# Layer 0's projections in float32r halves, five buffers of exponentials, and the FFN's halves made in the attention's last quads

## The chip, the core and the metric

The kernel runs on one core of one Trainium2 chip. The metric is the device time of one execution in microseconds (us). Five engines work side by side and wait for each other by semaphores: TensorE (PE, matmuls and transposes, with its weight loads as PEld), VectorE (DVE), ScalarE (ACT), GpSimd (POOL), and SyncE (SP), which here only issues DMAs.

## The reference: what is computed

Two transformer layers over x with B = 8 sequences of S = 512 rows and D = 256 columns, 16 heads of 16:

```python
x = x + _L0_attn_ref(_layernorm(x), gamma, beta, w_qkv)      # causal attention
x = x + _L0_ffn_ref(_layernorm(x), w_gate, w_up, w_down)     # gated FFN, 704 wide, fp4-quantized
x = x + _L1_attn_ref(_layernorm(x), Wq, bq, Wk, bk, Wv, bv, Wo, bo)  # causal, window of 64
x = x + _L1_ffn_ref(_layernorm(x), w_gate, w_up, w_down)     # gated FFN, 768 wide, integer weights
```

In layer 0's attention, `xn = (x - mu) * rsqrt(var + eps) * gamma + beta` and `qkv = xn @ w_qkv.T`; then the softmax of causal scores, and the weighted sum of v. In layer 0's FFN inputs, weights and hidden rows are each quantized to fp4 by blocks of 16 with the block's largest value as scale. A small change of q, k or the FFN's input can tip a quantized value, so the kernel keeps nearly full fp32 precision.

## The kernel before

x stays in SBUF for the whole kernel as eight tiles X[b] of 128 x 4 x 256. The work falls into an opening (0 to 38 us in the profiled execution), layer 0's attention (38 to 500), layer 0's FFN (to 797), layer 1's attention (to 1100) and layer 1's FFN.

**Attention.** `attention()` (line 360) gives an `opening` and a `body`. A batch is two units m (eight heads each), a unit two quads g of four heads: 32 quads. The loop of line 775 goes over the quads i, with r = i % 4 the quad of the batch. A quad of layer 0 has six positions p. At each, in this order, the loop emits one tile of the scores of quad i + 2 (`scores`: matmuls of lines 501 and 506 into a PSUM pair s, DVE's maximum in line 517), one tile of the transposed scores of quad i (`Outputs.causal`: matmuls of line 609 into a PSUM pair t, ACT's exponential in line 620 into a buffer "ex", POOL's causal selection in line 128), and what `at(p, ...)` has put beside it:

- the sums of ex with the values, line 674: key blocks 2 and 3 of the quad before at p1 = 1, key blocks 0 and 1 of this quad at f3 = 5; ACT's copy oT (695), the transposes pot (702), and x's update (1003, 1005);
- per batch, at r = 0 the values v (`values`) and the statistics of batch c + 2, at r = 1 its normalization y (168), at r = 2 its transposition (`turned`, `spin0`, `transposed`: PE 185, ACT 196 with gamma and beta as scale and bias into yT), at odd r the projections q and k of a later unit (`load_q`, `load_k` through `pieces`), and their ways through HBM (`stores`, `land`);
- the rows of maxima (567, 577, 578).

`step()` gives a turn to a filler in 3 of 10 calls: `before_ffn` quantizes layer 0's FFN weights (220 to 282), transposes them (884, 901), prepares the FFN's input of batch 0, and as its last steps splits gate weights, up weights and that input into halves (967 to 970). What is left of it runs after the loop.

PE's matmuls and transposes of the attention are pinned: their order is that in which the code emits them. The other engines' orders come from a scheduler that puts instructions by estimated times; pools with a number of buffers decide when a tile may be written again. All ex tiles of layer 0 share NX = 6 buffers, a quad has six of them. psum1 tiles share two buffers of one PSUM bank, psum2 tiles three pairs.

**Projections.** `project` (297) is two fp32 matmuls (one for each 128 rows of the contraction); each runs as two passes of 128 columns of weights in the profile, so q and k take four passes of 512 columns for a unit, v four of 256 for each 128 rows. Layer 1, from its second batch, uses the halves: a number is split in a float32r high part and a float32r rest, and `PAIRS` multiplies high x high, high x low and low x high, one pass each.

**Units' tiles.** `units_tiles` (349) makes a unit's q and k tiles and copies rows of constants (`own`) into k (353) on DVE; it is called twice in the opening and once in each `body`.

**Layer 0's FFN** begins with `wd_halves` (1204 to 1211): ACT copies the high half of the down weights (128 x 1536), POOL subtracts (line 1209). It then goes over 32 tiles of 128 rows; `prepare(1)` makes the input of batch 1 (`normed`: statistics, then ACT's fy in line 168).

Of the kernel before, what the change touches and what calls it, by code (L numbers as in the profile page):

```python
# [19 lines left out]
P = 128  # L20
# [7 lines left out]
NX = 6  # L28
# [18 lines left out]
def tile_two_layers(  # L47
# [51 lines left out]
    qkv_raw = wp.tile([P, NE, 3 * D], F32, tag="raw", name="qkv_raw")  # L99
    w3 = w_qkv_t.rearrange("(c p) f -> p c f", p=P)  # L100
    for i in range(3):
        nc.scalar.dma_start(qkv_raw[:, :, i * D : (i + 1) * D], w3[:, :, i * D : (i + 1) * D])
# [74 lines left out]
    def transposed(dst, src, tag, cs=range(NE), cols=None, pinned=False):  # L177
# [4 lines left out]
        for c in cs:  # L182
# [7 lines left out]
            if low is not None:  # L190
                nc.scalar.copy(dst[:, c, :], pt)
                nc.vector.tensor_tensor(low[:, c, :], pt, dst[:, c, :].bitcast(F32), ALU.subtract)
            elif cols is None:
                evacuate(dst[:, c, :], pt)
            else:
                nc.scalar.activation(
                    dst[:, c, :], pt, AF.Identity, bias=cols[1][:, c : c + 1],
                    scale=cols[0][:, c : c + 1],
                )

    def quantize(pool, dst, src, rows, nb, tag, exact):
# [29 lines left out]
        else:  # L231
# [15 lines left out]
            q8, pr = tmp("q8", BF16), tmp("pr")  # L247
# [49 lines left out]
    def project(dst, lhs, rhs):  # L297
# [3 lines left out]
        for l, r in pairs:  # L301
            for e in range(NE):
# [46 lines left out]
    def units_tiles(pool, n, what):  # L349
# [3 lines left out]
        nc.vector.tensor_copy(  # L353
# [4 lines left out]
    QK = [units_tiles(qk, n, "both") for n in range(2)]  # L358

    def attention(home, banded, stats, norm, spin, wq_s, wk_s, wv_s, qcol, kcol, bv_bc, post, filler):  # L360
# [11 lines left out]
        def halved(i, b, w):  # L372

            return [x[:, i] for x in FINE["qkv"]] if banded and b else [w]
# [26 lines left out]
        def pieces(b, m, w, col, name):  # L401
# [3 lines left out]
            project(pp, [x[:, :, m * P : (m + 1) * P] for x in ws], xT[b])  # L405
# [63 lines left out]
        def turned(b, c):  # L469
            if c == 0:  # L470
                fine = banded and b
# [4 lines left out]
                if fine:  # L476
# [267 lines left out]
        def body():  # L744

            q, k = units_tiles(home[0], 2, int(banded))
# [27 lines left out]
            ending = filler(home[0]) if banded else None  # L774
            for i in range(len(quads) + (2 if banded else 1)):
# [49 lines left out]
                if cur and not banded:  # L825
                    at(f3, lambda: cur.sums((0, 1)))
# [6 lines left out]
                for p in range(max(len(ts), nT if last or done else 0)):  # L833
# [10 lines left out]
                    if banded and i > 4 * B - 6:  # L844
# [4 lines left out]
            for _ in ending or ():  # L849
                pass  # L850
# [99 lines left out]
    def before_ffn(pool):  # L950
# [7 lines left out]
        pool.release()  # L958
        high = HALVES["pool"] = tc.alloc_tile_pool(name="halves", bufs=1, side="right")
        for t, nm, homes in (  # L960
            (wg1, "wg", (high, high)), (wu1, "wu", (high, high)), (YT[0], "y", (wp, wp)),
        ):
# [506 lines left out]
```

## Time and profile before

| | us |
|---|---|
| runs: median (lowest to highest) | 1281.98 (1281.46 to 1284.03) |
| profiled execution, whole | 1288.33 |
| its span | 1286.5 |
| layer 0's attention, 38 to 500: PE busy | 403.2 of 462 |
| the same: DVE, ACT, POOL busy | 376.3, 274.4, 239.7 |
| mean granted clock of PE | 0.954 of full speed |

A line of the timeline reads: start, duration of the group, engine, line of the code, operation, result <- operands, tile sizes and type, how many in a row, and in brackets how long the engine stood idle before it and what ended that. A "wait" line names the engine, what it was about to do, and the work whose end released it. Matmuls overlap, so that the time of a block of passes is best read from the start of its first to the start of PE's next work.

### The profile page before, as it was taken

What the parts mean: (1) busy time and instruction counts of PE and PEld (TensorE: products, weight loads), DVE (VectorE), ACT (ScalarE), POOL (GpSimd) and SP (SyncE); (2) the same over time, 40 slices, a digit from 0 to 9 for tenths busy, and PEclk for the clock granted to TensorE, in tenths of its full rate; (3) what the DMA queues carried; (4) which work ended last, traced back from release to release, by engine and by line L of the source; (5) the groups of instructions that cost most, each with busy time, mean ns of one, the idle gap of its engine ahead of it and who ended that gap; (6) DMA issues with size and microseconds to landing.
All of it is one profiled execution on the core that took longest, in us unless ns stands there. A gap on an engine that the chain in (4) does not pass through costs nothing. (4 is left out here: it accounts for less than half of the span.)

```text
span 1286.5 us, 27214 instructions
## 1 busy us (share of the span) xinstructions
PE 1100.3 (86%) x10910; PEld 819.8 (64%) x10910; DVE 943.5 (73%) x1603; ACT 659.7 (51%) x1008; POOL 698.8 (54%) x821
## 2 busy tenths in 40 slices
PE   4778989788998888788888887788998898889998
PEld 2444444444554445787888777567777776668887
DVE  4699896698788885789799857677776686545553
ACT  3255656465674676444444333455555554455553
POOL 5165564465445566655555533576766675534443
PEclk9899999898998999899999988899999998999999
DMA  8644334443453311000000025476675676000001
GB/s 229 140 96 87 86 74 86 79 94 67 91 116 74 81 18 50 1 1 1 1 1 1 1 72 105 100 165 155 144 149 125 141 164 163 2 1 33 33 26 43
DMA packets 51634, 99.53 MB, mean 77 GB/s; under 512 B 6702, under 2 KB 43568, under 8 KB 44848
## 3 DMA queue, kind: packets, MB, share of 16 engines
q1 hardware_dynamic: 50624, 96.96, 33.9%
q8 instruction: 88, 1.44, 0.5%
q10 hardware_dynamic: 816, 0.79, 0.2%
q14 instruction: 42, 0.34, 0.1%
q0 software_dynamic: 64, 0.00, 0.0%
HBM read 61.02 MB, written 29.36 MB: 70 GB/s over the span
## 5 line engine op out<-in xcount | busy, mean ns | idle before, releaser
L128 POOL TENSOR_SCALAR_AFFINE_SELECT ex<-ex 64x512 f32<-64x512 f32 (+2 forms) x448 | 268.9, 603 | 226.1 <-ACT ex L620 131.3
L620 ACT ACTIVATE ex<-t 128x1024 f32<-128x1024 f32 (+1 forms) x192 | 167.9, 882 | 125.3 <-PE t L609 114.1
L517 DVE TENSOR_REDUCE mx<-s 128x2 f32<-128x1024 f32 (+2 forms) x192 | 196.7, 1036 | 41.1 <-PE s L506 40.3
L1319 POOL TENSOR_TENSOR hT<-gh,hT 128x512 fp32r<-128x512 f32 x48 | 61.6, 1290 | 89.6 <-ACT hT L1318 66.1
L655 ACT ACTIVATE ex<-t 128x1024 f32<-128x1024 f32 x64 | 65.5, 1023 | 86.6 <-PE t L647 81.9
L501 PE MATMUL s<-kk_both,qq_both 96*128 96x512 bf16 (+3 forms) x352 | 84.6, 323 | 20.8 <-DVE mx L517 10.9
L506 PE MATMUL s<-cmask,minus_b 128*128 128x128 bf16 (+2 forms) x352 | 90.4, 257 | 0.0
L540 DVE TENSOR_REDUCE mx<-s 128x8 f32<-128x1024 f32 x64 | 77.6, 1215 | 15.3 <-PE s L535 15.2
L282 POOL TENSOR_TENSOR h<-h,sc_h 128x704 f32<-128x704 f32 x32 | 45.1, 1410 | 79.4 <-DVE h L281 73.6
L674 PE MATMUL po<-ex,vp 128*32 128x512 f32 (+3 forms) x1024 | 83.4, 442 | 1.3 <-DVE kr L418 1.3
L609 PE MATMUL t<-qq_both,kk_both 108*128 108x512 bf16 (+3 forms) x352 | 70.9, 306 | 9.1 <-ACT ex L620 4.7
L1386 DVE SCALAR_TENSOR_TENSOR gh<-ggu,gsl 128x512 f32<-128x512 f32 x48 | 33.2, 691 | 57.1 <-ACT gsl L1384 56.6
L1260 PE MATMUL pd<-wd_high,hT 128*128 128x256 f32 x384 | 61.7, 299 | 11.6 <-DVE hT L1251 7.0
L277 ACT ACTIVATE mg_h<-h 128x704 bf16<-128x704 f32 x32 | 25.2, 788 | 82.7 <-POOL h L229 82.7
L1227 PE MATMUL gu<-wg_wgh,fyT 128*128 128x352 f32 x224 | 65.3, 333 | 2.4 <-DVE h L1234 2.4
L501 PEld LDWEIGHTS <-qq_both 96*128 96x128 bf16 x352 | 33.0, 103 | 51.6 <-issue 38.0
L229 POOL TENSOR_TENSOR h<-h,rc_h 128x704 f32<-128x704 f32 x32 | 46.4, 1449 | 34.1 <-DVE rc_h L228 18.8
L1260 PEld LDWEIGHTS pd<-wd_high,hT 128*128 128x128 f32 x384 | 53.7, 200 | 16.4 <-DVE hT L1251 10.7
L1227 PE MATMUL gu<-wu_wuh,fyT 128*128 128x352 f32 x224 | 62.7, 322 | 0.0
L1375 PE MATMUL ggu<-yT,wg_r 128*128 128x512 f32 x192 | 57.6, 412 | 2.1 <-DVE yT L1319 1.1
L279 DVE SCALAR_TENSOR_TENSOR h<-mg_h,h 128x704 f32<-128x704 bf16 x32 | 40.6, 1269 | 22.4 <-ACT mg_h L277 22.4
L674 PEld LDWEIGHTS po<-ex,vp 128*32 128x32 f32 x1024 | 27.1, 109 | 43.9 <-issue 29.8
(335 smaller groups left out, 3167.9 us busy)
## 6 DMA issues: line engine op xcount, KB each, us to landing
q_hbm<-qp SPq DMA_DIRECT2D x90, 128.0 KB
k_hbm<-kp SPq DMA_DIRECT2D x90, 128.0 KB
qq_both<-q_hbm SPq DMA_DIRECT2D x44, 256.0 KB
kk_both<-k_hbm SPq DMA_DIRECT2D x22, 384.0 KB
qq_both<-q_hbm SPq DMA_DIRECT2D x44, 128.0 KB
kk_both<-k_hbm SPq DMA_DIRECT2D x22, 256.0 KB
qq<-q_hbm SPq DMA_DIRECT2D x20, 256.0 KB
vq<-vp SPq DMA_DIRECT2D x8, 512.0 KB
```

Of the source, the lines that this page charges most:

```text
L128: nc.gpsimd.affine_select(out=t, in_=t, compare_op=ALU.is_ge, fill=0.0, base=base, pattern=[[0, n] for n in shape[1:-1]] + [[sign, shape[- ...
L501: pin(nc.tensor.matmul(bank[:, a * w : (a + 1) * w], lhsT=q[:KF, hs[j], t * P : w], rhs=k[:KF, hs[j], :w], start=(a == 0), stop=False, ski ...
L506: pin(nc.tensor.matmul(bank.rearrange("p (i k) -> p i k", k=w)[:, :, t * P :], lhsT=minus_b, rhs=cmask[:, : len(part), :], start=False, st ...
L517: nc.vector.tensor_reduce(dst, src, AX.X, ALU.max)
L540: nc.vector.tensor_reduce(mx[:, t2 : t2 + 2, :], sc.rearrange("p t (j k) -> p t j k", k=P), AX.X, ALU.max)
L609: pin(nc.tensor.matmul(bank[:, a * w : (a + 1) * w], lhsT=k[: KF + 12, self.hs[j], t * P : (t + 1) * P], rhs=q[: KF + 12, self.hs[j], t * ...
L620: nc.scalar.activation(ex[:, :banks, :used], sc[:, :banks, :used], AF.Exp, scale=QSCALE)
L655: nc.scalar.activation(ex, sc, AF.Exp, scale=QSCALE)
L674: pin(nc.tensor.matmul(self.o[HP * j : HP * (j + 1), t * P :], lhsT=vp[:, t, 4 * c + j, :], rhs=self.ex[t, j], start=(t == 0), stop=(t == ...
L1227: nc.tensor.matmul(gu[:, i, :352], lhsT=YT[b][l][:, e, t * P : (t + 1) * P], rhs=w[r][:, e, f], start=(n == 0), stop=(n == 3 * NE - 1),)
L1260: nc.tensor.matmul(pd[:, :D], lhsT=hT[l][:, k, :], rhs=wd_halves[r][:, k, :], start=(l == r == k == 0), stop=(l == 1 and k == NH - 1),)
L1319: engine.tensor_tensor(lo, src, hi.bitcast(F32), ALU.subtract)
```

## The change

Names and sizes in the diff: KF = 96 rows of a unit's tiles, "raw" a place of the weights' pool that held `qkv_raw`.

- The qkv weights come into three ex buffers and are split into float32r halves in the opening (ACT copies, DVE subtracts). `transposed` writes the scaled and shifted block to a full tile, copies its high half (ACT) and subtracts (POOL; for batch 0 DVE). The projections of layer 0 then take three pairs, with q's and k's low half of the input last (`last`; in layer 1 too).
- NX goes from 6 to 5, and the quantizer's q8 shares the buffer of mg.
- The sums of key blocks 0 and 1 go from position f3 = 5 to f2 = 4.
- The constants' rows are copied by ACT in the opening and by POOL in `body`, in both layers.
- The FFN's halves become a generator `ffn_halves` of their own. It is stepped at positions 2 and 5 of the quads from i = 27, and its first step runs the filler to its end. It makes the down weights' low half too, in three pieces.

```diff
-NX = 6
+NX = 5
...
-    qkv_raw = wp.tile([P, NE, 3 * D], F32, tag="raw", name="qkv_raw")
-    w3 = w_qkv_t.rearrange("(c p) f -> p c f", p=P)
-    for i in range(3):
-        nc.scalar.dma_start(qkv_raw[:, :, i * D : (i + 1) * D], w3[:, :, i * D : (i + 1) * D])
...
-            if low is not None:
+            if low is not None and cols is not None:
+                full = cols[2]()
+                nc.scalar.activation(
+                    full, pt, AF.Identity, bias=cols[1][:, c : c + 1], scale=cols[0][:, c : c + 1]
+                )
+                nc.scalar.copy(dst[:, c, :], full)
+                cols[3].tensor_tensor(low[:, c, :], full, dst[:, c, :].bitcast(F32), ALU.subtract)
+            elif low is not None:
...
-            q8, pr = tmp("q8", BF16), tmp("pr")
+            q8, pr = tmp("mg", BF16), tmp("pr")
...
-    def project(dst, lhs, rhs):
+    def project(dst, lhs, rhs, last=False):
...
         for l, r in pairs:
+            if last:
+                l, r = r, l
...
-    def units_tiles(pool, n, what):
+    def units_tiles(pool, n, what, copy=nc.vector.tensor_copy):
...
-        nc.vector.tensor_copy(
+        copy(
             k[KF:].bitcast(F32), own[KF:].unsqueeze(2).to_broadcast([32, 8, S // 2])
         )
...
-    QK = [units_tiles(qk, n, "both") for n in range(2)]
+    QK = [units_tiles(qk, n, "both", nc.scalar.copy) for n in range(2)]
...
-            project(pp, [x[:, :, m * P : (m + 1) * P] for x in ws], xT[b])
+            project(pp, [x[:, :, m * P : (m + 1) * P] for x in ws], xT[b], True)
...
-                fine = banded and b
+                fine = not banded or b
...
-                if fine:
+                if not banded:
+                    xT[b].append(home[0].tile([P, NE, S], F32R, tag="yT0", name=f"yTl_{b}", bufs=1))
+                elif b:
                     xT[b].append(FINE["x"])
...
-            q, k = units_tiles(home[0], 2, int(banded))
+            q, k = units_tiles(home[0], 2, int(banded), nc.gpsimd.tensor_copy)
...
-            ending = filler(home[0]) if banded else None
+            ending = last_weights(home[0])
...
-                    at(f3, lambda: cur.sums((0, 1)))
+                    at(f2, lambda: cur.sums((0, 1)))
...
-                    if banded and i > 4 * B - 6:
+                    if i > 4 * B - 6 and (banded or p % 3 == 2):
                         next(ending, None)
...
+        qkv = [
+            wp.tile([P, 3, NE, D], F32R, tag=f"raw{n}", name=f"qkv_{n}") for n in ("", "l")
+        ]
+        for i in range(3):
+            full = ap.tile([P, 2, 512], F32, tag="ex", name=f"qkv_{i}", bufs=NX)[:, :, :D]
+            nc.scalar.dma_start(
+                full, w_qkv_t[:, i * D : (i + 1) * D].rearrange("(c p) f -> p c f", p=P)
+            )
+            QKV.append([wqkv[:, i] for wqkv in qkv])
+            halved.append((QKV[i], full))
+
+        def split_weights(i):
+            (high, low), full = halved[i]
+            nc.scalar.copy(high, full)
+            nc.vector.tensor_tensor(low, full, high.bitcast(F32), ALU.subtract)
...
         def spin0(b, c, dst):
-            transposed(dst, Y[b], f"a{b}", [c], (gcol, bcol), True)
+            if b == 0:
+
+                for i in range(3) if c == NE - 1 else ():
+                    split_weights(i)
+
+            def full():
+                return ap.tile([P, S], F32, tag="rem", name=f"yf_{b}_{c}")
+
+            engine = nc.gpsimd if b else nc.vector
+            transposed(dst, Y[b], f"a{b}", [c], (gcol, bcol, full, engine), True)
+
+        def ffn_halves(pool):
+
+
+            for _ in fill:
+                pass
+            wqp.release()
+            high = HALVES["pool"] = tc.alloc_tile_pool(name="halves", bufs=1, side="right")
+            for t, nm, homes in (
+                (wg1, "wg", ((high, "wgh"), (high, "wgl"))),
+                (wu1, "wu", ((high, "wuh"), (wp, "rawl"))),
+                (YT[0], "y", ((wp, "wg1"), (wp, "wu1"))),
+            ):
+                hi, lo = HALVES[nm] = [
+                    h.tile(list(t.shape), F32R, tag=tag, name=f"{nm}_{tag}") for h, tag in homes
+                ]
+                for e in range(NE):
+                    nc.scalar.copy(hi[:, e], t[:, e])
+                    nc.gpsimd.tensor_tensor(lo[:, e], t[:, e], hi[:, e].bitcast(F32), ALU.subtract)
+                    yield
+            YT[0] = HALVES["y"]
+            low = HALVES["wd"] = wp.tile([P, NH, D], F32R, tag="raw", name="wd_low")
+            for k in range(0, NH, 2):
+                hi = pool.tile([P, 4, D], F32R, tag="y", name=f"wd_high_{k}", bufs=1)[:, :2]
+                nc.scalar.copy(hi, wd1[:, k : k + 2])
+                nc.gpsimd.tensor_tensor(
+                    low[:, k : k + 2], wd1[:, k : k + 2], hi.bitcast(F32), ALU.subtract
+                )
+                yield
...
         wd_halves = [
-            wp.tile([P, NH, D], F32R, tag="raw", name="wd_high"),
-            fp.tile([P, NH, D], F32R, tag="wdl", name="wd_low", bufs=1),
+            fp.tile([P, NH, D], F32R, tag="wdh", name="wd_high", bufs=1), HALVES["wd"]
         ]
         nc.scalar.copy(wd_halves[0], wd1)
-        nc.gpsimd.tensor_tensor(
-            wd_halves[1], wd1, wd_halves[0].bitcast(F32), ALU.subtract
-        )
```

## The prediction

> **What bounds the kernel now.** I read the page's busy shares and slices first, then the stages' windows, PE's waits, and last the rows of the projections.
>
> ```profile
> PE 1100.3 (86%) x10910; PEld 819.8 (64%) x10910; DVE 943.5 (73%) x1603; ACT 659.7 (51%) x1008; POOL 698.8 (54%) x821
> PE   4778989788998888788888887788998898889998
> DVE  4699896698788885789799857677776686545553
> ```
>
> PE is the busiest engine, but few slices of layer 0's attention (slices 2 to 15, 32 us each) are full, and DVE comes close behind. The windows say it for the stage from 38 to 500 us (columns: time, then busy us of PE, its weight loads, DVE, ACT, POOL):
>
> ```profile
> 38.00:500.00 462.00, 403.23 (x2994) 220.14 (x2994) 376.34 (x631) 274.35 (x384) 239.68 (x322) 0.94 0.38 80
> ```
>
> PE works 403.2 of 462 us (87%). So PE work that goes is mostly time saved, and the 59 us in which PE stands still are the second thing the change can move. What ends them (us in total, times, longest):
>
> ```profile
> PE s L501 <- DVE mx L517: 17.2, 17, 3.3
> PE t L609 <- DVE mx L517: 9.8, 16, 1.8
> PE t L609 <- ACT ex L620: 9.7, 9, 3.6
> PE pot L702 <- ACT oT L695: 8.6, 6, 4.0
> ```
>
> DVE's maximum reduces free the score buffers too late (27 us), and ACT's exponentials and copies come late (18 us). That is a chain through three engines with PE's order written by hand; no wait is on a load of the weights.
>
> **Part 1: the projections, six passes of halves for four of fp32.** The old passes in layer 0, and the new kind as layer 1 already has it:
>
> ```profile
> 263.60 1.88 PE L303 MATMUL pk<-yT,qkv_raw 128*128 128x512 f32 x4
> 265.32 0.39 PE L501 MATMUL s<-kk_both,qq_both 96*128 96x128 bf16 x4
> ...
> 898.01 0.74 PE L303 MATMUL pq<-yT,qkv_wg 128*128 128x512 f32 x2
> 898.59 0.63 PE L303 MATMUL pq<-room,qkv_wg 128*128 128x512 f32 x2
> 899.05 0.62 PE L303 MATMUL pq<-yT,qkv_wu 128*128 128x512 f32 x2
> 899.54 0.66 PE L702 MATMUL pot<-ident,oT 128*128 128x128 f32 x4
> ```
>
> From the first pass to the next work of PE: 265.32 - 263.60 = 1.72 us before, 899.54 - 898.01 = 1.53 us in halves. Over all blocks of the trace the medians are 1.72 against 1.53 (q), 1.72 against 1.59 (k), 1.73 for eight passes against 1.53 for twelve (v). A batch has two of each: 2 x (0.19 + 0.13 + 0.20) = 1.04 us; seven batches lie in the loop: 7.3 us of PE. Bounds: the passes of one block in layer 1 follow each other in 0.235 us (512 columns) and 0.119 us (256), so six blocks without any start-up loss would gain 6 x 0.31 = 1.8 us a batch, 12.8 us. On the other side, a weight load of these lines lasts 0.188 us; if loads set the pace, twelve take 2.26 us against 1.73, which is +0.53 for each v block, and with q and k still gaining 0.64 a batch the part would cost 7 x 0.42 = 2.9 us. I take the measured blocks, 7.3, since it is the same shape on the same engine. Not all of it comes through: where DVE or ACT is the late one, a shorter block only makes the wait longer. The share of PE's busy time, 0.87, is the upper end; with 27 of 59 idle us ended by DVE I take 0.75: **-5.5**.
>
> A rule speaks against this part. The Trainium skill, "Perfetto Trace Analysis", section "Identifying the Most-Contended Engine", would have TensorE judged by the busy share of its weight loads and not of its matmuls; the change raises layer 0's from 32 to 48 loads a batch, and by 0.188 us each that is 3 us a batch, about 21 us slower. The rows of layer 1 disagree: twelve loads and passes went through in 1.53 us, so the loads overlap.
>
> **Part 2: the price of the halves of yT.** Before, one ACT pass (L196, 0.77 us) moved a transposed block out of PSUM; after, the pass writes a full copy, ACT copies its high half (a 128x512 copy is 0.58 to 0.63) and POOL subtracts (128x512 in f32, 1.16 to 1.27; in batch 0 DVE, 0.68). Per batch ACT +1.2, POOL +2.5 us; ACT is busy 59% and POOL 52% of the stage, so most of it lies beside PE. What doesn't:
> - The wait. PE's order has pq pinned soon after the transposes. In batch 2 the transposes end at 97.13, ACT's pass at 98.17, pq starts at 99.81: 1.64 us of room. The added copy, subtract and hops need 0.6 + 1.25 + 0.2 = 2.05; but x-low comes last, four passes or 1 us after pq's start. So it fits when POOL is free (room 2.6), and when POOL is in a select (0.41 to 0.70) or a product of the quantizer (1.92 at 256.07) it is late. Behind the waiting pass stand all the scores and tiles of PE. Ends: 0, and 2.5 us a batch; I take 0.3, by the selects: 6 x 0.3 = **+1.8**. At the loop's start (50 to 54 us) pq follows the transposes at once (51.82, with yT ending at 52.49), nothing covers the chain: 2.05 less what the passes hide: **+1.8** (0 to 4).
> - ACT's 1.2 us delays exponentials; with 18 us of PE's waits ended by ACT in 274 busy us, 7 x 1.2 more cost 8.4 x 18/274 = 0.6, twice that at the worst: **+1.0**.
>
> **Part 3: opening (0 to 38 us).** DVE's copies of own rows, one of them from 8.13 to 9.79, go to ACT and POOL. DVE's statistics then end earlier, and y, which starts at 14.62 after an ACT that stood still 9.77 us, at some 12.8. Against it: the extra ACT passes (+1.2) and three splits of weights beside it. Six passes save again. The first scores at 38.51 wait for k's way through HBM, which keeps its length. **-1.0** (-2 to +1).
>
> **Part 4: five buffers, sums one position earlier.** The first half of a quad's sums (16 passes) needs four exponentials, and it then stands before the sixth tile, which takes the buffer that it frees: no new wait by count. Their 1.7 us of passes now stand ahead of the sixth tile, where PE waited 0.4 to 1.2 us in about ten quads, 6 us in all, and no longer ahead of the next quad's scores. I take half: **-3** (-4 to +2, if the fourth exponential is late and the sixth tile with it).
>
> **Part 5: the FFN's halves.** The same six copies (ACT) and subtracts (POOL) move from after the loop's last steps into the last five quads; the down weights' low half, one POOL subtract of 3.51 us at 501.93 beside which a DVE instruction stretched to 2.16 us, becomes three pieces of 0.6 (ACT) and 1.2 (POOL) in the loop. What is freed at FFN0's start is 1.4 to 1.8 us of DVE; but the ACT copy of the high half (1.48 us) now stands right ahead of the normalization of batch 1 on ACT: **-0.3** (-1.8 to +1.5).
>
> **Part 6: layer 1's start (797 to 805 us).**
>
> ```profile
> 797.97 2.51 DVE L353 COPY kk<-own 32x2048 f32<-32x2048 f32 x1
> ...
> 804.71 1.22 PE L303 MATMUL pq<-yT,qkv_wg 128*128 128x512 f32 x2 [3.68 <-DVE room L192]
> ```
>
> The copy stands on DVE ahead of the reduces, the rows of maxima and the low half of x (room), for which PE waits 3.68 us. It goes to POOL (2.5 us earlier), and x-low is read two passes later (0.5). What comes next is ACT's high half, so not all: **-3** (-3.7 to 0).
>
> **Part 7: the order.** The scheduler moves the quantizer's steps. In the changed order one quad (batch 4, third quad) has between two of DVE's reduces some 8.4 us of other work, with batch 6's statistics, two waits for POOL and the transposes behind y; before has such a place at 293 to 305, where 13 us held 8.64 us of PE. After such gaps PE also runs slower: from 238 to 262, with PE idle 3.34 and 3.97 us, the granted clock was 0.81. The old jams stay or go by accident: **+1.5** (-3 to +6).
>
> **Sum:** -5.5 + 1.8 + 1.8 + 1.0 - 1.0 - 3 - 0.3 - 3 + 1.5 = -6.7 us. The profiled execution took 1288.3 us (span 1286.5), so 1281.6 there. It is 6.35 us above the median of the runs (1281.98), which makes **1275.3**.
>
> **Rivals.**
> 1. No change: the stage is set by the DVE chain (81% busy, 27 us of PE's waits), so PE's savings only lengthen waits: part 1 gives 0, and the sum is -1.2: 1281. For it: every slice's DVE digit of 6 to 9; against it: PE is busy 87% and has the fewest idle us.
> 2. Much faster: passes at their spacing (12.8 x 0.87 = 11.1), all of part 4 (-4), no order cost, yT's wait covered except at the start: -11.1 + 1.8 + 1.0 - 1 - 4 - 0.3 - 3 = -16.6: 1265.
> 3. Slower: yT's low half on POOL is the new wait of every batch. It queues behind two selects or a product (1.2 to 1.9 us) and PE stands behind the pinned pass. At 2.5 us a batch it is 15 in place of 1.8: -6.7 + 13.2 = +6.5: 1288. It decides from 0.3 + 6.7/6 = 1.4 us a batch. For it: DVE and POOL both wait for each other around y (mr_a took 1.89 us beside a POOL product at 256.13); against it: room of 2.6 us.
>
> **How the numbers follow.** Forecast (1271 to 1279) 0.42, rival 2 and beyond 0.18, rival 1 0.16, rival 3 0.24. Runs of this kernel tell 0.2% (2.6 us) from no change. The forecast and rival 2 are faster (0.60); rival 1 mostly the same (0.14 of 0.16), the rest with rival 3 slower (0.26). The range leaves out the far halves of both ends: 1263 to 1289.
>
> **What would show it.** Right: blocks of six in layer 0 at 1.5 to 1.6 us; the loop 5 to 10 us shorter between 38 and its end; PE's waits for the sixth tile gone; no PE wait for room at layer 1's start above 1.2 us. Wrong: a PE wait "pq or pk for POOL yTl" that sums over 8 us, an 8 us hole in batch 4, blocks of 2 us, or waits for the maxima that grow by what part 1 saved.

## The result, and the profile after

The changed kernel takes 1287.1 us (median of 12 runs, 1283.6 to 1295.2), the kernel before 1282.2 (12 runs, 1275.6 to 1284.0): a ratio of 1.0046, 95% interval 1.0028 to 1.0064. It is 3.6 to 8.2 us slower where I forecast 6.7 us faster. The busy times of the changed kernel:

```profile
PE 1095.3 (85%) x11038; PEld 829.4 (65%) x11038; DVE 940.8 (73%) x1604; ACT 677.2 (53%) x1032; POOL 723.4 (56%) x839
```

PE has 5 us less to do, ACT and POOL 18 and 25 us more. In the window of layer 0's attention it shows most clearly:

```profile
38.00:500.00 462.00, 396.50 (x3076) 225.51 (x3076) 376.34 (x631) 282.63 (x399) 265.78 (x338) 0.93 0.39 81
```

PE was busy 403.2 us there and is now 396.5; DVE is as busy as it was. A part of these 6.7 us is only the window, in which all now comes later. Between the same instructions (first exponential of the first and of the last quad, 56.55 to 491.71 us before and 61.16 to 494.31 now) PE was busy 379.5 us and is now 374.6: 4.9 less, in a time that is 2.0 us shorter. PE's waits, 40 to 495 us (the 9.8 us for k belong to the opening; before, this wait of 8.5 us ended ahead of 40):

```profile
PE s L504 <- DVE mx L520: 18.9, 17, 4.0
PE t L612 <- DVE mx L520: 10.4, 10, 3.7
PE s L504 <- DMA kk_both<-k_hbm: 9.8, 1, 9.8
PE pt_a L181 <- ACT y L164: 8.9, 1, 8.9
PE t L612 <- ACT ex L623: 7.3, 16, 1.8
...
PE pq L304 <- ACT yT L191: 2.0, 5, 1.4
PE pq L304 <- POOL yTl L192: 1.7, 6, 0.4
```

Whole spans mislead here: both profiled executions of the kernel before took 1288 us, 6 over its median, with 294 and 295 us in layer 1's attention, where the others took 286 to 291 (less and more, below: 296 and 298). So I cut each trace at the same instructions. The table gives us from the span's start to the first exponential of layer 0, on to the first exponential of the 32nd quad ("loop"), to the FFN's first gate, through the FFN's gates, to layer 1's first exponential, through its exponentials, and to the end. The last columns are the medians of the runs and the ratio to the kernel before on the same chip.

```
kernel         first  loop   to FFN  FFN    to L1  L1 att.  rest    median   ratio (95%)
before          56.5  435.2   13.6  274.1   33.9   293.6   179.5    1282.2
before_again    56.6  434.8   13.6  274.1   33.9   294.9   178.5
after           61.2  433.2   16.2  272.8   31.4   289.3   179.9    1287.1   1.0046 (1.0028-1.0064)
after_again     61.2  434.5   16.2  272.8   31.4   289.9   179.5
stats_early     60.3  435.8   16.2  271.9   28.8   287.6   179.5    1284.3   1.0010 (0.9986-1.0033)
fp32_proj       54.8  437.9   16.2  271.8   28.8   291.2   180.1    1281.5   0.9970 (0.9952-0.9988)
only_sums       57.0  437.4   14.8  274.8   33.5   287.8   179.6    1287.0   1.0022 (1.0001-1.0044)
sums_late       62.5  436.7   14.9  272.7   31.5   286.3   180.3    1287.0   1.0019 (0.9997-1.0040)
open_fp32       58.6  436.6   16.2  272.4   31.4   286.0   179.9    1284.1   1.0005 (0.9987-1.0022)
early_stats     53.3  436.0   16.2  271.9   28.8   290.9   179.8    1278.0   0.9953 (0.9931-0.9975)
less            52.3  437.9   16.2  272.9   31.5   296.2   180.0
more            53.4  437.9   16.2  271.9   28.8   297.6   180.1
fp32_early      53.0  433.4   16.2  270.4   28.8   286.9   181.0    1272.5   0.9910 (0.9884-0.9937)
best2           52.0  435.8   13.6  273.2   31.3   289.1   179.9    1279.3   0.9953 (0.9932-0.9975)
dve_more        51.9  437.3   16.2  271.7   29.8   291.0   179.9
rows_pool       50.1  435.0   16.2  272.3   31.5   286.6   180.2    1277.9   0.9949 (0.9927-0.9972)
best3           52.0  430.4   13.6  272.3   29.7   287.0   180.6    1270.0   0.9900 (0.9870-0.9930)
fe_sums_late    51.0  430.8   14.9  270.9   29.1   289.0   180.5    1267.4   0.9886 (0.9853-0.9920)
best4           51.5  425.3   13.6  272.9   31.4   287.4   179.2    1264.8   0.9860 (0.9823-0.9897)
before_early    52.8  432.0   13.6  274.4   34.0   287.2   179.5    1277.0   0.9951 (0.9928-0.9975)
```

Kernels whose loop has the same order tell the loop's own scatter: 433.2, 434.5 and 436.6 (after, after_again, open_fp32), 436.0 and 435.8 (early_stats, best2), 433.4 and 430.4 (fp32_early, best3). Differences of less than 3 us between two loops tell nothing by themselves.

By stages the change costs 4.6 us up to the first exponential, gains nothing that can be told in the loop (1.2, mean of two executions each), costs 2.6 at the passage to the FFN, gains 1.3 in it and 2.5 ahead of layer 1. That is +2.2 us, where the runs say 3.6 to 8.2; the rest I cannot place (layer 1's attention differs too much between executions).

### The profile page after: what moved, and what is told of

Its sections match the earlier page's. It is cut to its first block, busy times and chain, and to the rows that moved or that the text cites. A ratio compares the mean times of both kernels' runs of the same rounds, so it can differ in the third digit from the quotient of the medians.

```text
span 1283.9 us, 27524 instructions
## 1 busy us (share of the span) xinstructions
PE 1095.3 (85%) x11038; PEld 829.4 (65%) x11038; DVE 940.8 (73%) x1604; ACT 677.2 (53%) x1032; POOL 723.4 (56%) x839
## 4 chain that ended last, share of the span: by engine, by line
PE 40%; DVE 26%; POOL 13%; ACT 10%; DMA 6%; issue 5%; SPq 0%; ACTq 0%; POOLq 0%; DVEq 0%
PE ggu L1412 6%; DVE mx L520 6%; PE gpd L1384 3%; PE po L677 3%; PE t L612 3%; PE s L504 3%; POOL h L227 3%; POOL ex L124 3%; DVE h L277 2%; PE pv L304 2%; PE pk L304 2%; PE pq L304 2%; PE gu L1264 2%; PE pp L1120 2%; PE s L529 2%
## 5 line engine op out<-in xcount | busy, mean ns | idle before, releaser
L124 POOL TENSOR_SCALAR_AFFINE_SELECT ex<-ex 64x512 f32<-64x512 f32 (+2 forms) x448 | 272.6, 610 | 199.0 <-ACT ex L623 112.3
L504 PE MATMUL s<-kk_both,qq_both 96*128 96x512 bf16 (+3 forms) x352 | 83.0, 317 | 20.5 <-DVE mx L520 10.5
L543 DVE TENSOR_REDUCE mx<-s 128x8 f32<-128x1024 f32 x64 | 77.6, 1215 | 14.9 <-PE s L538 14.8
L677 PE MATMUL po<-ex,vp 128*32 128x512 f32 (+3 forms) x1024 | 87.6, 456 | 0.9 <-POOL ex L124 0.9
L1297 PE MATMUL pd<-wd_high,hT 128*128 128x256 f32 x384 | 61.7, 299 | 11.6 <-DVE hT L1288 6.9
L559 DVE TENSOR_TENSOR mx<-mx 128x16 f32<-128x16 f32 x128 | 56.1, 438 | 2.7
```

What stands on the lines that cost most here:

```text
L124: nc.gpsimd.affine_select(out=t, in_=t, compare_op=ALU.is_ge, fill=0.0, base=base, pattern=[[0, n] for n in shape[1:-1]] + [[sign, shape[- ...
L504: pin(nc.tensor.matmul(bank[:, a * w : (a + 1) * w], lhsT=q[:KF, hs[j], t * P : w], rhs=k[:KF, hs[j], :w], start=(a == 0), stop=False, ski ...
L543: nc.vector.tensor_reduce(mx[:, t2 : t2 + 2, :], sc.rearrange("p t (j k) -> p t j k", k=P), AX.X, ALU.max)
L677: pin(nc.tensor.matmul(self.o[HP * j : HP * (j + 1), t * P :], lhsT=vp[:, t, 4 * c + j, :], rhs=self.ex[t, j], start=(t == 0), stop=(t == ...
L1297: nc.tensor.matmul(pd[:, :D], lhsT=hT[l][:, k, :], rhs=wd_halves[r][:, k, :], start=(l == r == k == 0), stop=(l == 1 and k == NH - 1),)
```

## The experiments

**The hole, the halves and the sums.** Theory J: the 8 us stretch of DVE in batch 4 (the hole) and the start cost what the rest gained. Rivals: the halves of yT (H), the moved sums (S).

stats_early, statistics two quads earlier:

```diff
-                if r == 0 and c + 2 < B:
+                if banded and r == 0 and c + 2 < B:
                     at(f3, lambda: stats(c + 2))
+                if not banded and i == 0:
+                    at(f3, lambda: stats(2))
+                if not banded and r == 2 and c + 3 < B:
+                    at(f1, lambda: stats(c + 3))
```

> The changed kernel, with the statistics of a batch emitted two quads earlier (third quad of the batch three before, instead of the first quad of the batch two before). In the order that results, batch 6's statistics stand no longer on DVE between the down weights' quantization and the normalization, so that the third quad of batch 4 has no stretch of 8 us on DVE. Theory J (the jam): the profile of the changed kernel lost 8.9 us of PE there and ran slower for some us after it, so this kernel is 8 to 11 us faster than the changed kernel: 1276 to 1279, a ratio to the kernel before of 0.995 to 0.998. Rival H (the halves of yT and their chain through ACT and POOL are what costs): the hole is filled but time is lost in every batch, 1284 or more, ratio above 1.001. Rival S (the moved sums): also 1284 or more.

Measured 1284.3. The hole is gone; in the changed kernel, PE and DVE around it:

```profile
331.05 1.95 PE L181 MATMUL pt_a<-ident,y 128*128 128x128 f32 x4 [8.88 <-ACT y L164]
```
```profile
323.60 0.87 DVE L219 TENSOR_REDUCE am_wd<-raw_d 128x44 f32<-128x704 f32 x1
...
329.01 1.34 DVE L158 SCALAR_TENSOR_TENSOR mr_a<-mv_a,rs_a 128x4 f32<-128x4 f32 x1 [0.92 <-POOL rs_a L156]
```

and the same stretch, 319 to 346 us, with early statistics:

```profile
PE t L612 <- DVE mx L520: 2.5, 3, 1.5
PE pt_a L181 <- DVE on L1051: 1.6, 1, 1.6
```

The 8.9 us are there and go, but the loop does not get shorter (435.8 against 433.2 and 434.5): the quad with the hole shrank from 23.2 to 16.1 us, another, in batch 5, grew from 16.8 to 24.0. The first q block of batches 2 to 7, which waits for the halves (Part 2 below), also grew, by 5.7 us in all six, which is rival H's mechanism. Theory J's number did not come; what the hole alone costs is not separated from this. What the median gained stands behind the loop, in stages where the granted clock and transfers differ between executions.

fp32_proj puts the fp32 projections back and leaves all else changed:

```diff
-                fine = not banded or b
+                fine = banded and b
...
-            halved.append((QKV[i], full))
+            QKV.append([qkv[:, i]])
```

> The changed kernel with layer 0's projections as before: fp32 weights, fp32 yT by one ACT pass, four passes; sums, buffers, copies of own rows and the FFN's halves stay changed. The order that results has no stretch of 8 us on DVE in batch 4. Theory J: without halves the opening and the loop's start are 4 us shorter and the jam is gone, but seven batches pay 1 us each more: 1276 to 1282. It is then about as fast as the kernel with early statistics, within 4 us. Rival H: without the chain of the halves everything that the change lost comes back and the other edits' gains show: 1272 or less. Rival S: 1284 or more, as the changed kernel.

1281.5: within J's numbers. The loop is 3 to 5 us longer than the changed kernel's, but the first exponential comes 6.4 us earlier. So the larger part of the halves' price lies ahead of the loop. That they are free in it is not shown: their own blocks pay there too (Part 2 below).

only_sums is the kernel before with f2 in place of f3 for the sums; sums_late the changed kernel with f3.

> The kernel before with one edit: the sums of key blocks 0 and 1 one position earlier (six buffers). Theory J: it gains what my part 4 said or a little less, 1277 to 1282 (ratio 0.996 to 1.000). Rival S: the sums now wait for the fourth exponential, ratio 1.003 or more.

> The changed kernel with the sums back at the last position, with five buffers. The order that results still has the stretch of 8 us in batch 4. Theory J: no gain over the changed kernel; the sixth exponential of each quad must wait for a buffer until the sums behind its own tile have run, and PE's next tiles wait for it: 1290 to 1300. Rival S: the sums' place was the loss: 1283 or less.

only_sums: 1287.0, a ratio of 1.002 (1.000 to 1.004), the loop 2.2 us longer. Rival S has the sign right: no gain, rather a loss. sums_late came out as fast as the changed kernel or faster, against my expectation. PE's waits from 57 to 490 us, before and with only the sums moved:

```profile
PE s L501 <- DVE mx L517: 16.0, 15, 3.3
PE t L609 <- DVE mx L517: 9.8, 16, 1.8
PE t L609 <- ACT ex L620: 9.7, 9, 3.6
```
```profile
PE t L609 <- DVE mx L517: 18.6, 14, 4.2
PE s L501 <- DVE mx L517: 9.5, 12, 3.0
PE pv L303 <- ACT wu L888: 6.4, 1, 6.4
```

The waits for exponentials fell from 9.7 to 3.1 us, as meant. DVE's reduces ended 28.1 us instead of 25.8, and one wait for ACT's copy of transposed weights (wu) 6.4.

**The opening.** open_fp32: batch 0 in fp32, the weights split after the opening.

```diff
-                fine = not banded or b
+                fine = b
...
+            if not banded and not b:
+                return FULL[i]
...
         for _ in opening0():
             pass
+        for i in range(3):
+            split_weights(i)
```

> The changed kernel, but batch 0, which the opening projects, keeps fp32: one ACT pass into yT and four passes, straight from the weights as they land; the weights are split after the opening's projections. The order of the loop is that of the changed kernel, with the stretch of 8 us in batch 4. Profiles so far put the loop's first exponential at 56.6 us in the kernel before, 61.2 in the changed one, 54.8 in the one with fp32 projections throughout. Theory O (the opening pays for the halves: yf, copy and subtract stand in a row on the path to the first scores): the first exponential comes 2 us earlier than in the changed kernel, by the opening's share (40.5 against 38.5 us for the first scores), and the kernel is 2 us faster than the changed kernel: ratio 1.002 to 1.004. Rival H (the halves cost in every batch of the loop): no faster than the changed kernel, 1.004 or more.

The first exponential came 2.6 us earlier, at 58.6; the ratio fell from 1.0046 to 1.0005, more than forecast. Theory O has the sign, but the rows give its mechanism only a part of it. The first scores come at 39.66 instead of 40.54, 0.9 us earlier, and the changed kernel's second execution (after_again) had them at 39.44 without any edit. The other 1.7 us lie in batch 1's q and k behind them: the same twelve passes took 4.90 us in the changed kernel (from 55.07, granted clock 0.65) and 3.18 us here (from 54.25, clock 1.00; here DVE makes batch 1's low half, there POOL). Nor did the splits of the weights leave the opening: emitted behind it, they still ran on ACT at 4.35, 5.45 and 8.96 us. The halves stand in a row on the path to the first scores (changed kernel, PE):

```profile
18.52 0.80 PE L304 MATMUL pq<-yT,qkv__164 128*128 128x512 f32 x1 [0.67 <-ACT yT L191]
19.85 0.79 PE L304 MATMUL pq<-yT,qkv__164 128*128 128x512 f32 x1 [0.53 <-ACT yT L191]
...
40.54 0.59 PE L504 MATMUL s<-kk_both,qq_both 96*128 96x512 bf16 x1 [9.76 <-DMA kk_both<-k_hbm]
```

The first pass of 18.09 became 18.52, the second waits again, and the scores start at 40.54 instead of 38.51 (after_again and before_again: 39.44 and 38.61). That wait of 9.8 us is room for work. early_stats and before_early put batch 1's transposes and projections there; early_stats has open_fp32 and stats_early too, before_early is the kernel before with this edit alone:

```diff
+            if not banded:
+                norm(1)
             for u in units[:2]:
...
+            if not banded:
+                next_unit()      # turned(1, c), load_q, load_k and stores of units[2]
             for i in range(1 if banded else 0, 2):
                 for s in scores(i):
```

> The kernel with early statistics, with batch 0 in fp32, and with batch 1's transposes and first projections ahead of the first scores, where PE stands still for 8.5 to 9.8 us while q and k go through HBM. Theory O with J: the first exponential comes at 52 to 54 us instead of 60.3, the loop is as long as with early statistics, so 1277 to 1279 and a ratio of 0.994 to 0.997. Rival H: 1282 or more.

> The kernel before with batch 1's normalization, transposes and first projections ahead of the first scores, in PE's idle 8.5 us, and nothing else; the loop's order is kept. Theory O: the first exponential at 51 to 53 us instead of 56.6, the loop as before (435 us), ratio 0.995 to 0.998. Rival: what the loop's first quads gain they wait for later, 0.999 or more.

Both as expected: 1278.0 and 1277.0. In before_early PE works where it waited:

```profile
31.62 2.16 PE L303 MATMUL pq<-yT,qkv_raw 128*128 128x512 f32 x4
33.61 1.88 PE L303 MATMUL pk<-yT,qkv_raw 128*128 128x512 f32 x4
```

The first exponential comes 3.7 us earlier, and the loop keeps that lead (432.0, no longer than before).

**The same kernels once more.**

> The kernel before once more, for a second profile: its first one took 6 us more than the median. Theory N (what differs between executions is layer 1, where PE waits for transfers through HBM): layer 0's attention is the same within 1 us, and layer 1's attention takes 287 to 290 us instead of 293.7 from its first to its last exponential. Rival: the jams of layer 0's loop differ from execution to execution.

> The changed kernel once more, for a second profile. Theory N: first exponential at 61 us and the loop's length of 433 us from first to last quad within 1 us, the hole of 8.9 us ahead of the transposes of batch 6 again; what differs lies in layer 1.

Layer 0's loop repeats here within 1.4 us (0.4 in the kernel before), the hole too. Layer 1's attention of the kernel before did not fall to 290; theory N holds, nearly, for layer 0 only.

**Does PE's work count, and does DVE's?** less and more change the pairs of layer 0 in early_stats, fp32_early takes its halves away:

```diff
-        pairs = PAIRS if len(lhs) == 2 else ((0, 0),)
+        pairs = (PAIRS if FINE else PAIRS[:2]) if len(lhs) == 2 else ((0, 0),)              # less
+        pairs = (PAIRS if FINE else PAIRS[:2] + PAIRS[1:]) if len(lhs) == 2 else ((0, 0),)  # more
```

> The kernel of early_stats with only the first two of the three pairs in layer 0's projections of batches 1 to 7 (the low half of one operand is left out, so q, k and v lose precision). Each block is 2 (q, k) or 4 (v) passes shorter, 0.47 us by the spacing of the passes; six blocks in each of seven batches make 20 us of PE work less, of which 17 lie in the loop from quad 0 to quad 31 (six batches). Theory P (PE sets the loop, so that its work counts at its busy share, 0.87): the loop is 422 us instead of 436. Theory D (the chain through DVE's reduces, ACT and the order set the loop, and PE's savings turn into waits): 431 us or more.

> The kernel of early_stats with one pair taken twice in layer 0's projections of batches 1 to 7 (so that a low part is added twice and values are slightly wrong): 20 us more PE work in all, 17 in the loop. Theory P: the loop is 450 us instead of 436. Theory D: the added passes are hidden in PE's waits in part, 440 to 446.

> The kernel of early_stats with fp32 projections in all batches of layer 0: early statistics, batch 1's transposes and projections ahead of the first scores, everything else changed. Against early_stats it has no halves of yT in the loop and 1 us more of passes a batch. Theory P: the loop is 4 to 6 us longer than the 436 us of early_stats, the first exponential as early, ratio to before 0.998 to 1.001. Theory D: the loop is within 2 us of 436 and the kernel as fast as early_stats, 0.994 to 0.997: the halves gain nothing in the loop.

The loop's windows of early_stats, less and more (PE is the first busy time, DVE the third):

```profile
53.00:489.00 436.00, 377.11 (x2949) 214.96 (x2948) 362.62 (x614) 271.66 (x385) 257.90 (x325) 0.94 0.38 79
```
```profile
52.00:490.00 438.00, 357.01 (x2840) 200.30 (x2839) 370.69 (x610) 270.10 (x385) 258.41 (x325) 0.93 0.39 79
```
```profile
53.00:491.00 438.00, 386.91 (x3057) 230.74 (x3056) 359.25 (x614) 272.08 (x385) 257.33 (x325) 0.96 0.37 78
```

With PE 20 us less busy the loop is 1.9 us longer, with PE 10 us more busy 1.9 us longer too: no change either way, by the loop's scatter. The granted clock (0.94, 0.93, 0.96) moved with the work: busy time times clock gives 354, 332 and 371 us, so that by this estimate some 22 us of work went and some 17 came, and the faster clock gave 7 of them back in more. Theory P's numbers, 422 and 450 us, did not come. In less, PE's waits for the reduces took it all:

```profile
PE t L618 <- DVE mx L526: 39.6, 22, 10.2
PE s L510 <- DVE mx L526: 17.4, 13, 3.6
```
```profile
207.38 1.01 PE L618 MATMUL t<-qq,kk 108*128 108x512 bf16 x2 [10.17 <-DVE mx L526]
```

where early_stats had 11.6 and 17.8. But two single waits, of 10.2 and 8.0 us (at 207 and 271 us), are 18.2 of these 57.0, and early_stats has none above 3.7: between two reduces DVE had steps of the weights' quantizer. The two quads with them are 12.6 us longer than in early_stats, the other 29 together 10.7 us shorter. So less does not tell whether PE's work counts for nothing or counts and was lost again to a moved order.

And fp32_early is not slower but faster than early_stats (loop 433.4, ratio 0.991): the halves gain nothing in this order. In early_stats the first q block of batches 2 to 7 takes 2.70 to 4.70 us, with PE's waits for POOL's low half at 5.6 us; in fp32_early it takes 1.72 to 1.82. Then DVE alone: dve_more makes the copy of the maxima's rows twice, rows_pool gives it to POOL, both on fp32_early:

```diff
+                nc.vector.tensor_copy(rows[:, 2:4], rows[:, 0:2])     # dve_more: a second time
-                nc.vector.tensor_copy(rows[:, 2:4], rows[:, 0:2])     # rows_pool
+                nc.gpsimd.tensor_copy(rows[:, 2:4], rows[:, 0:2])
```

> The kernel of fp32_early with one copy more on DVE for each quad: the copy of two heads' rows of maxima (12 x 1024, 0.42 us) is made twice in layer 0, 32 x 0.42 = 13.4 us of DVE work, 13 of it in the loop, none on PE. Theory D (DVE's chain sets the loop): DVE's work counts nearly in full, the loop from quad 0 to quad 31 is 443 to 447 us instead of 433.4. Theory P: DVE has room (358 busy us of 436), the loop grows by 3 us or less.

> The kernel of fp32_early with the same copy moved from DVE to POOL in layer 0: 13.4 us less on DVE, somewhat more on POOL (busy 238 of 436). Theory D: the loop is 5 to 12 us shorter than 433.4, ratio to before 0.983 to 0.988. Rival: POOL's copy stands behind selects and the next tile's rows come later, the loop is as long or longer, 0.990 or more.

The windows of fp32_early, dve_more and rows_pool:

```profile
53.00:486.00 433.00, 381.46 (x2838) 204.27 (x2838) 358.22 (x610) 264.37 (x373) 235.78 (x313) 0.96 0.38 79
```
```profile
52.00:489.00 437.00, 378.89 (x2809) 203.94 (x2838) 376.25 (x641) 265.14 (x373) 235.25 (x313) 0.95 0.38 79
```
```profile
50.00:485.00 435.00, 382.84 (x2811) 204.33 (x2839) 345.40 (x581) 265.35 (x373) 268.02 (x345) 0.95 0.38 79
```

DVE 18 us busier: 3.9 us longer. DVE 13 us less busy: 1.6 us longer, or no change. So theory D, as a chain in which DVE's load counts in full, did not come either. No load of one engine that I varied moved the loop as it should have. What is left is the handoffs between the engines in the order that each of them has; every edit shifted that order too, so that this is argued and not shown by an experiment of its own.

**The moved sums and the buffers.** fe_sums_late is fp32_early with the sums at f3; best4 has NX = 6 again and best2's later copy.

> The kernel of fp32_early with the sums of key blocks 0 and 1 back at the last position, with five buffers. My part 4 put the move at -3 us (-4 to +2). If the move is worth that, the loop is 3 us or more longer than 433.4 here; five buffers with late sums also make the sixth exponential wait for the sums ahead of it, some us more: 436 to 441. If the sums' place is hidden behind DVE: 431 to 435.

> The kernel of fe_sums_late (fp32 projections, early statistics, batch 1's transposes and projections ahead of the first scores, late sums) with six buffers of exponentials again and the copy of the down weights' high half behind the FFN's first tile. Late sums with six buffers are the loop of the kernel before, with its statistics earlier: 428 to 431 us, the passage to the FFN 12.5 to 13.6. Ratio to before 0.985 to 0.989. If five buffers cost nothing and the passage is given back in the FFN: as fe_sums_late, 0.987 to 0.990.

Late sums do not make the loop longer, as I expected, but shorter by 2.6 us (430.8): their move gained nothing here either. (In the changed kernel, with halves, it is the other way: 436.7 with late sums against 433.2 and 434.5. Both are about the scatter.) With five buffers they make ACT wait, which a sixth buffer ends. ACT's waits in fe_sums_late and best4:

```profile
ACT ex L619 <- PE t L608: 90.7, 108, 5.3
ACT ex L619 <- PE po L673: 24.9, 24, 1.8
```
```profile
ACT ex L619 <- PE t L608: 112.8, 110, 4.8
```

24 waits for sums, 24.9 us of ACT, are gone, and ACT's waits for tiles are 22.1 us more. The loop is 5.5 us shorter, 425.3, the shortest of all, in one execution each and at a granted clock of 0.96 instead of 0.94; the runs' intervals of the two kernels overlap. best4 takes 1264.8 us, a ratio of 0.986 (0.982 to 0.990), and beats both kernels. It keeps of the change the copies of own rows, the shared buffer of q8, x-low last in layer 1 and the FFN's halves in the attention.

**The passage to the FFN.** best2 (on early_stats) and best3 (on fp32_early) copy the down weights' high half behind the first tile and put the last quad's sums back behind the sixth tile.

```diff
-        nc.scalar.copy(wd_halves[0], wd1)
...
+                if n == 0:
+                    nc.scalar.copy(wd_halves[0], wd1)
...
-                    at(f2, lambda: cur.sums((0, 1)))
+                    at(f2 if i < 4 * B - 1 else f3, lambda: cur.sums((0, 1)))
```

> The kernel of early_stats with two edits at the passage to layer 0's FFN: the copy of the down weights' high half is emitted behind the first tile's work instead of ahead of batch 1's normalization, and in the last quad alone the sums go back behind the sixth tile. The time from the last quad's first exponential to the FFN's first gate was 13.6 us before and 16.2 in the changed kernel; by the two readings of that passage (the normalization 1.5 us behind the copy, the last output 1.2 us late behind the sums) it goes back to 13.6, and the kernel is 2.5 us faster than early_stats: ratio 0.992 to 0.995. Rival: what follows waits for something else (rows of the FFN's second tile), no change, 0.995 to 0.997.

> The kernel of fp32_early with best2's two edits of the passage to the FFN (high half of the down weights copied behind the first tile's work, the last quad's sums behind the sixth tile). The passage goes from 16.2 to 13.6 us; in best2 that was given back in the FFN and ahead of layer 1. Expected: given back here too in part, ratio 0.988 to 0.992.

The passage is 13.6 us again in both. In best2 the FFN and what follows up to layer 1 are 3.8 us longer than in early_stats. 2.5 of these lie ahead of layer 1, the stage that differs by 2.6 us between kernels whose code there is the same, with PE's granted clock (last section): that the edits gave them back is not shown. In best3 the runs gained 0.001, within the intervals. What happened at the passage in the changed kernel, on ACT:

```profile
505.72 1.48 ACT L1248 CAST wd_high<-wd 128x1536 fp32r<-128x1536 f32 x1 [2.47 <-POOL x L1049]
507.10 2.07 ACT L164 ACTIVATE fy<-x,mr_f,rs_f 128x256 f32<-128x256 f32 x4
```

## Why the prediction was wrong, point by point

By stages, forecast and measured in the profiles: +0.8 and +4.6 us up to the first exponential; -4.2 and -1.2 in the loop (parts 1, 4, 7 and the loop's share of part 2); -0.3 and +1.3 from there through the FFN; -3 and -2.5 ahead of layer 1. So 3.8 us of the miss lie at the start and 3.0 in the loop; 2.8 us between the profiles' +2.2 and the runs' +5.0 stay unplaced. Three steps failed:

- the start's sum, +0.8 for the halves' chain with nothing beside it, where +4.6 were measured;
- in part 2, the room of 1.64 us ahead of q, which part 4 of the same change takes away: 0.9 us a batch instead of 0.3;
- "PE work that goes is mostly time saved": where PE's blocks did come out as short as forecast (sums_late), the loop was no shorter.

The parts one by one:

- **Bounds.** PE's busy share of 0.87 did not make its saved work time. My waits table shows who took it: DVE and ACT ended the waits, and in less, with 20 us less of PE, DVE's reduces end 57.0 us of them instead of 29.4. Whether that lies in the loop itself or in the orders that moved with each edit stays open.
- **Part 1 (-5.5).** The blocks were right where nothing in them waits: in the changed kernel the next work starts 1.56 us after the first of these passes, the medians are 1.58 (k) and 1.59 (v) against 1.59 and 1.53 forecast. Half of the q blocks wait inside (Part 2). Judged by its weight loads the kernel would have been 21 us slower, which did not happen.

```profile
167.17 0.71 PE L304 MATMUL pk<-yT,qkv__164 128*128 128x512 f32 x2
167.71 0.62 PE L304 MATMUL pk<-yT,qkv_l 128*128 128x512 f32 x2
168.17 0.62 PE L304 MATMUL pk<-yTl,qkv__164 128*128 128x512 f32 x2
168.73 1.07 PE L677 MATMUL po<-ex,vp 128*32 128x512 f32 x8
```

  No run here supports the factor 0.75. All q, k and v blocks of the attention together take 77.9 us before and 70.2 in sums_late, about the 7.3 less that I counted, and the loop there is 436.7 us; but it also has five buffers, for which ACT waits 22.5 us, and the hole. The change without its halves (fp32_proj) has a loop 3 to 5 us longer, early_stats without them (fp32_early) one 2.6 us shorter. Rival 1 had the mechanism of waits that grow; it expected 1281 because it kept my other terms.
- **Part 2, the wait in each batch (+1.8).** Too small: +5.2 (six first q blocks of 2.37 to 2.63 us against 1.59). The room of 1.64 us that I read in batch 2 is 1.65 in batches 2 to 7 of the kernel before, and what fills it is the sums of key blocks 0 and 1, between the transposes and q. Part 4 moves these 1.7 us ahead of the transposes. So q starts 0.5 to 0.6 us before yT is complete, and its first block of each batch stops for yT and again for its low half. Before, changed, and the changed kernel with the sums back (sums_late):

```profile
156.44 0.61 PE L185 MATMUL pt_a<-ident,y 128*128 128x128 f32 x4
156.97 1.71 PE L674 MATMUL po<-ex,vp 128*32 128x512 f32 x16
...
159.62 1.88 PE L303 MATMUL pq<-yT,qkv_raw 128*128 128x512 f32 x4
```
```profile
157.67 0.61 PE L181 MATMUL pt_a<-ident,y 128*128 128x128 f32 x4
...
159.25 0.50 PE L304 MATMUL pq<-yT,qkv__164 128*128 128x512 f32 x1
159.90 0.50 PE L304 MATMUL pq<-yT,qkv__164 128*128 128x512 f32 x1 [0.15 <-ACT yT L191]
...
161.27 0.51 PE L304 MATMUL pq<-yTl,qkv__164 128*128 128x512 f32 x1 [0.17 <-POOL yTl L192]
161.62 0.39 PE L504 MATMUL s<-kk_both,qq_both 96*128 96x512 bf16 x1
```
```profile
161.58 1.71 PE L677 MATMUL po<-ex,vp 128*32 128x512 f32 x16
...
164.03 0.81 PE L304 MATMUL pq<-yT,qkv__164 128*128 128x512 f32 x2
...
165.62 0.39 PE L504 MATMUL s<-kk_both,qq_both 96*128 96x512 bf16 x1
```

  In the changed kernel these six blocks take 2.37 to 2.63 us, in sums_late 1.58 or 1.59, and before 1.72: a loss where I counted a gain. The waits that the profile names, 2.3 us for yT and yTl from 60 us on, are less than half of the 5.2; the rest is passes that no longer follow each other closely. In early_stats and stats_early the same blocks cost more (2.70 to 4.71). Rival 3 had this mechanism and by luck the time, 1288: its price of 15 us did not come. The halves with late sums and six buffers no run has tried.
- **Parts 2 and 3, start and opening (+0.8 together).** Measured +4.6 to the first exponential: +2.0 to the first scores (+0.8 in the second executions), the rest behind them, where PE waits 1.44 us for batch 1's yT and then makes q and k at a granted clock of 0.65. I let y come at 12.8; it came at 14.40 (14.62 before; 13.42 in the second execution). ACT, which got the copies, first waits for the last weights that it splits, and copies until 14.12:

```profile
9.79 0.62 ACT L985 CAST qkv__164<-qkv 128x512 fp32r<-128x512 f32 x1 [3.82 <-DMA qkv<-in_L_attn_w_qkv_dram]
10.43 3.69 ACT L354 COPY kk_both<-own 32x2048 f32<-32x2048 f32 x2
14.40 2.07 ACT L164 ACTIVATE y<-x,mr_a,rs_a 128x256 f32<-128x256 f32 x4 [0.28 <-DVE mr_a L158]
```

  DVE's mr_a comes as late, at 14.21, behind the weights' low halves and a `minus_b` that lasts 1.91 us; either alone would have held y to about here. Without splits (fp32_proj) ACT copies from 5.04 on, and y starts at 10.56.
- **Part 4 (-3).** No gain shown: +2.2 (only_sums), +2.6 (fp32_early against fe_sums_late), -2.2 to -3.5 (the changed kernel against sums_late), all about the loop's scatter. In only_sums the covered waits came back in part as waits for the reduces. In the last quad the sums ahead of the sixth tile also delay the last exponential: 1.2 of the passage's 2.6 us.
- **Part 5 (-0.3).** +1.4 from the copy ahead of fy, as named, but the FFN got only 1.3 us back of all 2.6.
- **Part 6 (-3).** -2.5, about right: PE's wait for room fell from 3.68 to 1.70 (my sign said 1.2 at most). The stage's length also follows the granted clock (0.80 before, 0.84 in the changed kernel), so not all of it need be the wait.
- **Part 7 (+1.5).** The hole of 8.9 us stood where the order said. The loop is no shorter without it, but there the first q blocks take 20.5 us instead of 14.8 and a quad of batch 5 is 7.2 us longer: the hole's own price is not shown.

## What to carry to other kernels

Room that is read off the order of before holds only for that order: here one part of the change moved away the very work that another part counted on as cover. So write down the order with all edits in it, and look again at what then stands between a result and its reader.

A busy share of 87% does not say what an engine's saved work is worth while its waits are ended by engines that follow it. Vary its work alone, and then look whether the other engines' order stayed; here it did not, and the question stayed open. The gain that is shown by one edit alone lay in work moved into the one long wait for a transfer (before_early, 0.995). At the start there was little beside the added hops to cover them.

## What the runs showed of the hardware that I had not expected

- DVE's 128x128 `minus_b`, 0.36 us before, took 1.91 us beside a POOL copy of 1.98 us in the changed kernel's opening:

```profile
12.38 1.91 DVE L110 TENSOR_SCALAR minus_b<-ident 128x128 bf16<-128x128 f32 x1
```
```profile
12.23 1.98 POOL L354 COPY kk<-own 32x2048 f32<-32x2048 f32 x1
```

- At the FFN's end PE comes out of a pause of 3.7 us with a clock that differs between kernels whose code there is the same: in the changed kernel it was granted 0.50 from 790 to 795 us and 0.88 in the next 5, in early_stats 0.66 and 1.00 at the same place of the work (from 784 us). The stage up to layer 1 took 31.4 and 28.8 us.
